# Corner taps summed on VectorE, rank-one lots beside contractions, and row stores in threads of their own

## The chip, the cores and the metric

The kernel runs on one core of a Trainium2 chip. Its engines work side by side, each through its own instructions in their order: TensorE (PE in the profile; PEld are its weight loads), VectorE (DVE), ScalarE (ACT), GpSimd (POOL) and SyncE (SP), whose queue issues most DMAs. They wait for one another by semaphores. The metric is the device time of one execution in microseconds (us); the kernel before took 39103.82 us in the median of three runs (39095.82 to 39139.67).

## The reference, cut to what matters

Two layers on an image batch of 8 × 128 × 64 × 64. The first adds a deformable convolution of the group-normalised image: for each of nine taps, four corners of the image are gathered, weighted and summed, and the taps are contracted with the convolution's weights.

```python
v = g(y0i, x0i) * ((1 - wy) * (1 - wx))[None] + g(y0i, x0i + 1) * ((1 - wy) * wx)[None] \
    + g(y0i + 1, x0i) * (wy * (1 - wx))[None] + g(y0i + 1, x0i + 1) * (wy * wx)[None]
...
out = jnp.einsum('bckhw,ock->bohw', cols, weight.reshape(Cout, Cin, K2))
```

The second takes the 4096 pixels of each image as a sequence. After a layer norm it runs a state-space scan with a state of 256 × 256 (d, n) per image, then a mixture of eight experts of which each pixel uses two.

```python
deltaA = jnp.exp(jnp.einsum('bld,dn->bldn', delta, A))
deltaB = jnp.einsum('bld,bln->bldn', delta, Bv)

def step(state, inp):
    dA_i, dB_i, x_i, C_i = inp
    state = dA_i * state + dB_i * x_i[:, None, :]
    y = jnp.einsum('bdn,bn->bd', state, C_i)
    return (state, y)
```

All of it is float32.

## The kernel before, in words

**Ahead of the scan** the kernel normalises the images, computes the offsets, and writes the table of corners (`table`), the gather indices and corner weights (`recs`) and the images themselves (`xl`) to DRAM.

**The scan** goes over 4096 positions, for all eight images at once. Sixteen positions are a *block* (256 of them), two are a *chunk* (eight a block), and one is a *step*. A hardware loop of eight turns holds 32 blocks, written out by `scan_block`. Each step has 12 *slots*; what is emitted in a slot is written out by hand, and it fixes each engine's order.

The state is kept transposed, n on the partitions, as four *pairs* of images of 1024 elements a partition: pairs 0, 1 and 2 in SBUF (`ht`), pair 3 in PSUM (`ud`). A step does this:

- `product` (L960) multiplies the decay factors `et` by the state: on GpSimd for pairs 0 to 2, into the four buffers `mt` that are used in turn (`buf`, L956: product p of step j has buffer (3j + p) mod 4), and on VectorE for pair 3, into the one buffer `md`.
- `unit` (L943) makes delta · B · x on TensorE, as rank-one lots from `uu`, into the one PSUM tile `up` (pairs 0 to 2) or added later to pair 3's own `ud`. `add` (L967) is VectorE's sum of product and lot. A new lot for `up` waits until the addition has read the one before.
- `contract` (L974) contracts a product with C (`zc`) on TensorE, into `yp`, 16 records for two pairs. It reads the products and not the new state; what B contributes is put in at the end of the block (`qt` in `behind`, L750). A buffer of `mt` is free for a later product when its contraction has read it.
- `decay` (L913) makes the decay factors of the chunk after this one: 19 groups of bf16 matmuls from `rt` (rows of delta, split into three bf16 parts, laid out with zeros) and `alhs` (rows of A), each into one of the PSUM banks that turn, and ScalarE's exponential (L933) from there into `et`. The groups are spread over slots 0 to 20 of a chunk's 24.

At the start of a chunk SP's queue gets the loads of `uu` for the next chunk (L897, four DMAs) and of `rt` for the one after that (L888, one DMA of 1102.5 KB). Both come from DRAM, where the scan's operands were stored a block ahead.

**Between these** the work of other blocks is dealt out by *threads* (Python generators that yield a number of slots): `conv` (L548) for the block two ahead, `project` (L623) for the next one, and `behind` for the one before. In each slot `Work.step` (L477) lets a thread emit its next piece while the planned load of TensorE and of VectorE is under ROOM (7.0, 9.0); every slot takes RATE (3.2, 3.2) off that load, and each piece adds its `cost`. Three banks are shared: a thread takes one (`take`) and gives it back (`free`), and the decays turn over the rest. Every thread must have ended when the block in which it runs ends.

- `conv` gathers a tap's four corners by an indirect DMA on GpSimd's queue (L567), scales them on ScalarE (L588, four operations into `w`), and sums and transposes them at once on TensorE, by four matmuls with the identity that add up in one bank (L596). ScalarE copies the result to `vt` (L603). After nine taps come the convolution and the layer norm.
- `project` makes delta, B · x, C and the gate. The three bf16 parts of delta and of B · x are stored to `pr` (L671 and L722, 12 DMAs each), and those of delta as rows to `rz` (L698: three parts of ten groups of rows, 30 DMAs), all on SP's queue, each lot at the point of `project` where its data is ready, the rows ten to a slot.

The order of the queue at the change, per block: chunk 1 has `uu` and `rt`, then 12 stores of `dpt` and 30 of `dst`; chunk 2 has its loads only; chunk 3 its loads and the 12 stores of `bpt`.

Of the kernel before, what the change touches and what calls it, by code (L numbers as in the profile page):

```python
# [32 lines left out]
P = 128  # L33
# [35 lines left out]
RATE = (3.2, 3.2)  # L69
# [4 lines left out]
def kernel(  # L74
# [352 lines left out]
    md = fix.tile([P, 2, NH, DIN], FP, name="md")  # L427
# [42 lines left out]
    class Work:  # L470
# [77 lines left out]
    def conv(b0, l0, kt):  # L548
# [13 lines left out]
        vt = one.tile([P, TAPS + 1, P], FP, tag="bulk", name="vt")  # L562
# [14 lines left out]
        for j in range(2):  # L577
            gather(j)
            yield 4
        for j in range(TAPS):  # L580
# [4 lines left out]
            w = two.tile([P, 4 * P], FP, name="w")  # L585
            for q in range(4):
                c0 = TAPS + 4 * j + q
                nc.scalar.activation(  # L588
                    w[:, P * q : P * q + P], g[:, P * q : P * q + P], AF.Copy,
                    scale=rec[:, c0 : c0 + 1],  # L590
                )
                yield 1
            yield 1
            wk = yield from take()
            for q in range(4):
                nc.tensor.matmul(  # L596
                    wk[:, :P], w[:, P * q : P * q + P], ident,
                    start=(q == 0), stop=(q == 3),
                )
# [22 lines left out]

    def project(k):  # L623


        wk = yield from take()
# [10 lines left out]
        z = one.tile([P, DIN], FP, name="z")  # L637
# [31 lines left out]
        for p in range(QI // 2):  # L669
            for i in range(3):  # L670
                nc.sync.dma_start(  # L671
                    out=pr[k].rearrange("i j p w b l n -> i p w (b l) j n")[i, p, 1],
                    in_=dpt[32 * p : 32 * p + 32],
                )
        yield 1
# [17 lines left out]
        for i in range(3):  # L693
            for a in range(NA + 1):
                q = min(GD, P - GD * a)
                c0 = 3 * i * NCH * RROW
                c1 = c0 + 3 * NCH * RROW
                nc.sync.dma_start(  # L698
                    out=rz[k][:q, c0:c1].rearrange("q (m x) -> q m x", x=RROW)[
                        :, :, 2 * a * CT : 2 * a * CT + 2 * CT  # L700
                    ],
# [417 lines left out]
```

## Time and profile before

| what | us |
|---|---|
| median of three runs | 39103.82 |
| the profiled execution | 39033.45 |
| its span, first to last instruction | 39031.8 |
| of it, before the scan's first product | 1771.5 |
| ScalarE's exponentials, L933 (40980 of 518 ns) | 19952.0 busy |
| VectorE's additions, L969 (12288 of 1218 ns) | 14971.8 busy |
| TensorE's decay matmuls, L924 | 12481.6 busy |
| TensorE's contractions, L981 from `mt` | 9369.2 busy |
| TensorE's lots, L949 into `up` | 5013.7 busy |
| mean granted TensorE clock | 0.949 |

Busy time counts what overlaps within a row once, and rows of one engine can overlap one another. The time of 39031.8 is one execution's; the median of the runs is 70 us above it. The page's slices are alike from the third of forty on: the scan repeats one block 256 times, so the block is the unit in which its time can be read. DMA engines are busy for about three tenths throughout, at 100 GB/s. A row's last part, after the second bar, is the time in which the engine stood idle just ahead of such instructions, and what ended that.

### The profile page before, as it was taken

How to read it: one execution, taken by the hardware profiler on the slowest of the kernel's cores; microseconds unless marked ns; L12 is line 12 of the kernel's file. 1: busy time of each engine (PE TensorE's matmuls, PEld its weight loads, DVE VectorE, ACT ScalarE, POOL GpSimd, SP SyncE). 2: the span in 40 equal slices, each digit the busy share in tenths (PEclk: the TensorE clock that was granted, in tenths of full speed). 3: DMA queues.
4: the chain of work that ended last, by engine and by line, in shares of the span. 5: the costliest groups of instructions: out<-in, count | busy, mean ns of one | idle time of the engine just before them, and what ended most of it. 6: DMA issues, size and time to landing. Idle time of an engine off the chain costs nothing. (4 is left out here: it accounts for less than half of the span.)

```text
span 39031.8 us, 851601 instructions
## 1 busy us (share of the span) xinstructions
PE 31598.8 (81%) x324270; PEld 17751.1 (45%) x324270; DVE 27353.8 (70%) x35860; ACT 24136.3 (62%) x62725; POOL 31028.9 (79%) x14691
## 2 busy tenths in 40 slices
PE   3488888888888888888888888888888888888888
PEld 1244444444444444444444444444444444444444
DVE  1277777777777777777777777777777777777777
ACT  0166666666666666666666666666666666666666
POOL 0288888888888888888888888888888888888888
PEclk7799999999999999999999999999999999999999
DMA  3333333333333333333333333333333333333333
GB/s 87 77 101 102 101 100 101 101 101 102 101 99 102 102 100 101 101 101 101 102 99 100 102 102 101 100 102 101 101 103 101 102 101 102 102 99 102 103 102 98
DMA packets 4799907, 3906.80 MB, mean 100 GB/s; under 512 B 3351549, under 2 KB 4378966, under 8 KB 4536022
## 3 DMA queue, kind: packets, MB, share of 16 engines
q1 hardware_dynamic: 4529962, 3182.00, 29.1%
q0 software_dynamic: 185760, 608.85, 5.6%
q10 hardware_dynamic: 80072, 61.51, 0.6%
q8 instruction: 2532, 41.48, 0.4%
q14 instruction: 1581, 12.95, 0.1%
HBM read 3268.71 MB, written 582.10 MB: 99 GB/s over the span
## 5 line engine op out<-in xcount | busy, mean ns | idle before, releaser
L961 POOL TENSOR_TENSOR mt<-et,ht 128x1024 f32<-128x1024 f32 x12288 | 28707.8, 2367 | 5843.1 <-ACT et L933 2895.4
L933 ACT ACTIVATE et<-bank 128x448 f32<-128x448 f32 (+1 forms) x40980 | 19952.0, 518 | 10189.4 <-PE bank L924 9662.8
L969 DVE TENSOR_TENSOR ht<-mt,up 128x1024 f32<-128x1024 f32 x12288 | 14971.8, 1218 | 9770.2 <-PE ud L949 5277.8
L924 PE MATMUL bank<-rt,alhs 126*128 126x224 bf16 (+1 forms) x81960 | 12481.6, 258 | 3161.1 <-ACT et L933 1504.4
L924 PEld LDWEIGHTS <-alhs 126*128 126x128 bf16 x81960 | 6844.7, 100 | 9068.6 <-issue 7073.1
L981 PE MATMUL yp<-mt,zc 128*32 128x256 f32 x98304 | 9369.2, 405 | 0.0
L949 PE MATMUL up<-uu 32*128 32x256 bf16 x49152 | 5013.7, 277 | 2504.2 <-DVE ht L969 2271.0
L961 DVE TENSOR_TENSOR md<-et,ud 128x1024 f32<-128x1024 f32 x4097 | 4977.7, 1215 | 81.6 <-PE yp L981 57.5
L971 DVE TENSOR_TENSOR ud<-md,ud 128x1024 f32<-128x1024 f32 x4096 | 5005.2, 1222 | 0.0
L981 PEld LDWEIGHTS yp<-mt,zc 128*32 128x32 f32 x98304 | 3474.3, 113 | 3350.9 <-issue 1742.2
L981 PE MATMUL yp<-md,zc 128*32 128x256 f32 x32768 | 4520.8, 396 | 0.0
L949 PEld LDWEIGHTS <-uu 32*128 32x128 bf16 x65536 | 1858.8, 92 | 4900.8 <-issue 4660.2
L588 ACT ACTIVATE w<-g,rec 128x128 f32<-128x128 f32 x9288 | 3602.4, 404 | 122.5 <-DMA rec<-recs 113.3
L596 PE MATMUL bank<-ident,w 128*128 128x128 f32 x18576 | 2966.7, 289 | 262.8 <-ACT w L588 118.2
L596 PEld LDWEIGHTS bank<-ident,w 128*128 128x128 f32 x18576 | 2371.3, 191 | 941.4 <-ACT et L933 648.3
L567 POOL DMA_INDIRECT g<-table,rec x2322 | 2262.4, 974 | 494.0 <-issue 259.7
L949 PE MATMUL ud<-uu 32*128 32x256 bf16 x16384 | 1670.2, 282 | 206.0 <-DVE md L961 202.8
L981 PEld LDWEIGHTS yp<-md,zc 128*32 128x32 f32 x32768 | 1661.1, 111 | 0.0
L603 ACT COPY vt<-bank 128x128 f32<-128x128 f32 x2322 | 614.9, 265 | 1090.8 <-PE bank L596 1090.7
L859 ACT ACTIVATE se<-bank,gate 128x128 f32<-128x128 f32 x2048 | 768.2, 377 | 392.7 <-PE bank L852 359.1
L298 POOL MEMSET xpad<- 128x66 f32 x8 | 1.2, 153 | 1227.8 <-POOLq L265 1227.8
L852 PE MATMUL bank<-ew_sb,tn2t 128*128 128x256 f32 x2048 | 726.4, 439 | 170.3 <-ACT et L933 126.4
(200 smaller groups left out, 16168.0 us busy)
## 6 DMA issues: line engine op xcount, KB each, us to landing
rt<-rz SPq DMA_DIRECT2D x2050, 1102.5 KB
uu<-pr SPq DMA_DIRECT2D x8196, 36.0 KB
pr<-dpt SPq DMA_DIRECT2D x3084, 48.0 KB
pr<-bpt SPq DMA_DIRECT2D x3084, 48.0 KB
rz<-dst SPq DMA_DIRECT2D x6939, 21.0 KB
g<-table,rec POOLq DMA_INDIRECT x2322
rec<-recs SPq DMA_DIRECT2D x2064, 2.8 KB
table<-xtok SPq DMA_DIRECT2D x256, 128.0 KB
```

Of the source, the lines that this page charges most:

```text
L567: nc.gpsimd.indirect_dma_start(out=g, out_offset=None, in_=table, in_offset=bass.IndirectOffsetOnAxis(ap=rec.bitcast(I32)[:, j : j + 1], a ...
L588: nc.scalar.activation(w[:, P * q : P * q + P], g[:, P * q : P * q + P], AF.Copy, scale=rec[:, c0 : c0 + 1],)
L596: nc.tensor.matmul(wk[:, :P], w[:, P * q : P * q + P], ident, start=(q == 0), stop=(q == 3),)
L852: nc.tensor.matmul(wk[:, :DIN], tn2t, ew_sb[:, DIN * hf : DIN * hf + DIN], start=True, stop=True,)
L859: nc.scalar.activation(se[:, ex, :], wk[:, P * j : P * j + P], AF.Copy, scale=gate[:, ex : ex + 1],)
L924: nc.tensor.matmul(ps[:, m * (NH * f + h) : m * (NH * f + h + 1)].rearrange("p (q t) -> p q t", q=n), alhs[:KR, g + f, P * h : P * h + P], ...
L933: nc.scalar.activation(ec[:, :, :, P * f + d0 : P * f + d0 + n], ps[:, m * f * NH : m * (f + 1) * NH].rearrange("p (h d t) -> p h t d", h= ...
L949: nc.tensor.matmul((up if p < QP else ud)[:, r, h], uu[c % 2][rows, 0, b % 2, lo, P * h : P * h + P], uu[c % 2][rows, 1, b % 2, lo, :], st ...
L961: (nc.gpsimd if p < QP else nc.vector).tensor_tensor(buf(j, p), et[c % 2][:, lo, PAIRS[p][0] : PAIRS[p][1] + 1 : 2], ht[p] if p < QP else ...
L969: nc.vector.tensor_tensor(ht[p], buf(j, p), up, ALU.add)
L971: nc.vector.tensor_tensor(ud, md, ud, ALU.add)
L981: nc.tensor.matmul(yp[32 * (b // 2) : 32 * (b // 2) + 32, :DIN], zc[c % 2].rearrange("p s x -> p (s x)")[:, s0 : s0 + 32], buf(j, p)[:, r, ...
```

## The change

1. **Corner taps.** Of the nine taps, those with even number (five) are summed over their four corners by VectorE into `v` and transposed by one TensorE transpose. The odd ones keep their four matmuls. Two taps share a bank and one ScalarE copy, so there are five copies of `vt` and not nine. `vt` has a tile of its own.
2. **RATE** is (2.8, 3.2) and was (3.2, 3.2): TensorE's planned load is taken down more slowly, and background work is dealt out more thinly.
3. **Slots.** The lots of pairs 0 and 3 move from slot 3 to slot 2, ahead of the last step's contraction of pairs 1 and 2, which moves from slot 0 to slot 2 along with GpSimd's third product. The contraction of pairs 0 and 3 moves from slot 6, behind the lot of pair 1, to slot 9, behind the lot of pair 2. `md` has two buffers.
4. **Stores.** The stores of `dpt`, `dst` and `bpt` become threads, put ahead of the other threads three slots after their data is made; each issues three DMAs and yields three slots. Assertions check that a load is emitted only after all stores of what it reads. `z` and `bx` share one buffer.

```diff
-RATE = (3.2, 3.2)
+RATE = (2.8, 3.2)
...
-    md = fix.tile([P, 2, NH, DIN], FP, name="md")
+    md = several(2, [P, 2, NH, DIN], FP, "md")
...
+            while later:
+                self.threads.insert(0, [later.pop(0), slot])
...
+            ws[j] = two.tile([P, 4 * P], FP, name="w")
             for q in range(4):
...
+                if q == 1 and j % 2 == 1:
+                    nc.vector.tensor_reduce(
+                        v, ws.pop(j - 1).rearrange("p (q c) -> p c q", q=4), AX.X, ALU.add
+                    )
+                    cost(0, 5)
                 yield 1
+            if j % 2 == 0 and j + 1 < TAPS:
+                continue
+            n = 1 + j % 2
+            if n == 1:
+                yield 1
+                nc.vector.tensor_reduce(
+                    v, ws.pop(j).rearrange("p (q c) -> p c q", q=4), AX.X, ALU.add
+                )
+                cost(0, 5)
+                yield 2
             yield 1
             wk = yield from take()
-            for q in range(4):
-                nc.tensor.matmul(
-                    wk[:, :P], w[:, P * q : P * q + P], ident,
-                    start=(q == 0), stop=(q == 3),
-                )
-                cost(1)
-                if q == 1:
-                    yield 1
-            nc.scalar.copy(vt[:, j, :], wk[:, :P])
+            nc.tensor.transpose(wk[:, :P], v, ident)
+            cost(1)
+            if n == 2:
+                yield 1
+                w = ws.pop(j)
+                for q in range(4):
+                    nc.tensor.matmul(
+                        wk[:, P : 2 * P], w[:, P * q : P * q + P], ident,
+                        start=(q == 0), stop=(q == 3),
+                    )
+                    cost(1)
+                    if q == 1:
+                        yield 1
+            nc.scalar.copy(
+                vt[:, j + 1 - n : j + 1, :],
+                wk[:, : n * P].rearrange("p (t c) -> p t c", t=n),
+            )
...
+    def store_rows(k, dst):
+        yield LAG
+        for a in range(NA + 1):
+            q = min(GD, P - GD * a)
+            for i in range(3):
                 c0 = 3 * i * NCH * RROW
                 c1 = c0 + 3 * NCH * RROW
                 nc.sync.dma_start(
...
+            yield 3
+        there.add(("rows", k))
...
-                    if sl == 0:
+                    if sl == 2:
+                        unit(c, lo, (0, 3))
                         if last:
                             contract(*last.pop())
                         product(j, c, lo, 2)
                     elif sl == 3:
-                        unit(c, lo, (0, 3))
                         add(j, 0)
                     elif sl == 5:
                         add(j, 3)
                     elif sl == 6:
                         unit(c, lo, (1,))
-                        contract(j, c, lo, (0, 3))
...
                             product(*nxt, 3)
                         unit(c, lo, (2,))
+                        contract(j, c, lo, (0, 3))
```

`store_delta` and `store_b` have the same form as `store_rows`, with four rounds of three DMAs where that has ten.

More of the change, by code (lines that the diff above doesn't have):

```diff
@@ L561, in conv @@
         yield LOADS
-        vt = one.tile([P, TAPS + 1, P], FP, tag="bulk", name="vt")
+        vt = one.tile([P, TAPS, P], FP, name="vt")
         gs, ws = {}, {}
@@ L579, in conv @@
             yield 4
+        v = one.tile([P, P], FP, name="v")
         for j in range(TAPS):
@@ L636, in project @@
         yield 1
-        z = one.tile([P, DIN], FP, name="z")
+        z = one.tile([P, DIN], FP, tag="zb", name="z")
         nc.scalar.mul(z, wk[:, DIN:], 0.5)
@@ L668, in project @@
         free()
[L669 to L675, printed above, removed]
+        later.append(store_delta(k, dpt))
         dst = one.tile([P, 3, NCH, 2, CT], BF, name="dst")
@@ L692, in project @@
         free()
[L693 to L701, printed above, removed]
-                    in_=dst[GD * a : GD * a + q].rearrange("q j c f t -> q (j c) (f t)"),
-                )
-            yield 1
+        later.append(store_rows(k, dst))
+        yield 1
         wk = yield from take()
@@ L713, in project @@
         yield 1
-        bx = one.tile([P, DIN], FP, name="bx")
+        bx = one.tile([P, DIN], FP, tag="zb", name="bx")
         nc.scalar.copy(bx, wk[:, :DIN])
@@ L719, in project @@
         free()
-        for p in range(QI // 2):
-            for j in range(3):
-                nc.sync.dma_start(
-                    out=pr[k].rearrange("i j p w b l n -> j p w (b l) i n")[j, p, 0],
-                    in_=bpt[32 * p : 32 * p + 32],
-                )
+        later.append(store_b(k, bpt))
         yield 1
@@ L887, in load_r @@
     def load_r(k, c):
+        assert ("rows", k) in there
         nc.sync.dma_start(
@@ L895, in load_u @@
     def load_u(k, c):
+        assert ("delta", k) in there and ("b", k) in there
         for p in range(QI // 2):
@@ L1044, in run @@
             pass
+        while later:
+            run(later.pop(0))
     for b0 in range(0, NB, QI):
```

39 lines of the change are left out of this document (35 added, 4 removed).

## The prediction

> **What bounds it now.** I read the page first, then the waits, then one block of the scan cut at its eight chunks, then the queue that feeds it. Busy shares and three rows of the page:
>
> ```profile
> PE 31598.8 (81%) x324270; PEld 17751.1 (45%) x324270; DVE 27353.8 (70%) x35860; ACT 24136.3 (62%) x62725; POOL 31028.9 (79%) x14691
> L961 POOL TENSOR_TENSOR mt<-et,ht 128x1024 f32<-128x1024 f32 x12288 | 28707.8, 2367 | 5843.1 <-ACT et L933 2895.4
> L596 PE MATMUL bank<-ident,w 128*128 128x128 f32 x18576 | 2966.7, 289 | 262.8 <-ACT w L588 118.2
> L567 POOL DMA_INDIRECT g<-table,rec x2322 | 2262.4, 974 | 494.0 <-issue 259.7
> ```
>
> TensorE and GpSimd are both near 80%, so neither alone sets the time; the waits between them do:
>
> ```profile
> DVE ht L969 <- PE ud L949: 5277.8, 2864, 15.5
> POOL mt L961 <- ACT et L933: 2895.4, 1274, 32.5
> PE up L949 <- DVE ht L969: 2271.0, 3027, 1.9
> POOL mt L961 <- PE yp L981: 1284.1, 784, 6.0
> PE bank L924 <- DMA rt<-rz: 1256.3, 254, 11.7
> ```
>
> (Total us, times, longest.) Divided by 256 blocks, GpSimd loses 11.3 us a block to late decay factors (et) and 5.0 to a multiplicand buffer that TensorE has not read yet (yp); TensorE loses 8.9 to state additions that still hold `up`, and 4.9 to one load of `rt`. A block in the middle, its chunks from first product to first product (columns: us, then busy us of PE, PEld, DVE, ACT, POOL, TensorE clock, DMA share, GB/s):
>
> ```profile
> 22156.30:22173.50 17.20, 14.50 (x152) 8.14 (x151) 13.24 (x21) 11.43 (x30) 14.01 (x7) 1.00 0.29 82
> 22173.50:22191.60 18.10, 14.91 (x147) 7.86 (x147) 14.91 (x21) 10.86 (x26) 14.96 (x7) 0.91 0.39 115
> 22191.60:22208.50 16.90, 13.13 (x144) 6.56 (x143) 15.14 (x31) 10.53 (x26) 15.96 (x8) 1.00 0.54 87
> 22208.50:22231.70 23.20, 17.63 (x161) 9.05 (x162) 12.39 (x13) 12.78 (x34) 15.12 (x8) 0.85 0.45 137
> 22231.70:22250.70 19.00, 16.86 (x177) 10.61 (x176) 12.54 (x12) 12.82 (x35) 15.92 (x8) 1.00 0.33 99
> 22250.70:22268.30 17.60, 16.00 (x181) 9.28 (x179) 12.76 (x11) 14.16 (x40) 16.95 (x9) 1.00 0.36 112
> 22268.30:22283.80 15.50, 14.34 (x154) 9.48 (x154) 10.73 (x10) 11.67 (x31) 13.99 (x7) 1.00 0.28 92
> 22283.80:22299.80 16.00, 12.34 (x151) 7.04 (x149) 13.89 (x23) 9.70 (x24) 14.00 (x6) 1.00 0.25 82
> sum 143.50, PE 119.73 PEld 68.03 DVE 105.61 ACT 93.94 POOL 120.92; mean PE 14.97 PEld 8.50 DVE 13.20 ACT 11.74 POOL 15.12
> ```
>
> This block's 143.5 us stand for 256 (37225 us from the first product at 1771.5 to the end of the last, 145.4 each with the loop's turns). Six products keep GpSimd 14.0 us in every chunk; the chunks last 15.5 to 23.2. The worst, chunk 3, starts with the wait for `rt`. The timeline of the queue and of TensorE shows why:
>
> ```profile
> 22190.50 13.85 SPq L698 DMA_DIRECT2D rz<-dst  x30
> 22204.44 1.35 SPq L897 DMA_DIRECT2D uu<-pr  x4
> 22206.42 0.32 SPq L888 DMA_DIRECT2D rt<-rz  x1
> 22212.40 0.55 PE L924 MATMUL bank<-rt,alhs 126*128 126x224 bf16 x2 [4.34 <-DMA rt<-rz]
> ```
>
> Thirty row stores take SP 13.85 us; the loads that chunk 2 should issue first thing (22191.6) stand behind them, and `rt` is issued 14.8 us into the chunk. It lands some 6 us later (22206.42 to 22212.40), when TensorE has stood 4.34 us.
>
> **The change, part by part.** The sum is made per chunk. I count each engine's instructions between the first rank-one lots of successive chunks in the order in which they stand in both built programs, and price them by rows.
>
> *TensorE.* A 128-column float32 matmul is 0.32 us (L596: 2966.7 over 9288 matmuls of two records), a 256-column one 0.70 (L543, wb: 358.5 over 514). Background matmuls by chunk stand, narrow/wide, at 7/2, 6/0, 0/2, 12/4, 19/2, 12/0, 19/0, 1/2 before: 76 × 0.32 + 12 × 0.70 = 32.7 us. The scan's share is then 119.7 - 32.7 = 87.0, or 10.9 a chunk. Each of five taps loses four matmuls (2966.7/2322 = 1.28 us) for one transpose (L618: 84.8/258 = 0.33 us), so 4.7 us a block go. With RATE 2.8 the rest is spread: 7/2, 4/0, 7/2, 5/0, 4/6, 16/0, 16/0, 2/2. TensorE by chunk: 14.5, 12.8, 12.3, 17.5, 18.4, 14.7, 17.0, 12.6 before, 14.5, 12.2, 14.5, 12.5, 16.4, 16.0, 16.0, 12.9 after.
>
> *GpSimd.* 14.0 a chunk and 1.19 a gather ((2262.4 + 494.0)/2322). The nine gathers stand 0, 1, 2, 1, 2, 3, 0, 0 before and 0, 1, 4, 1, 2, 1, 0, 0 after, so chunk 2 rises to 18.8.
>
> *VectorE.* Five reductions of 512 elements a partition are new, and no row has one: a reduction of 256 (L747) is 0.425, an addition of 1024 (L969) 1.218; these are the ends. It is nearest to L747; on the line between them it is 0.69, so 3.4 us a block (2.1 to 6.1). Chunks 2 to 6, where they stand, have 1.8 to 10.8 us of idle VectorE before; the cover is there. Without it 3.4 × 256 = 880 us come on. The gate's small operations move into chunk 3, which then holds ten large ones (12.2), seventeen of about 0.21 and one reduction: 16.5, more than GpSimd's 15.2. Chunk 7 gets three small ones more: 13.9 + 0.7 = 14.6.
>
> [...]
>
> *The larger of the three engines,* chunk by chunk: before 14.5, 15.2, 16.4, 17.5, 18.4, 17.6, 17.0, 14.0, sum 130.6; after 14.5, 15.2, 18.8, 16.5, 16.4, 16.0, 16.0, 14.6, sum 128.0. The block took 143.5, so 12.9 were waits: by chunk 2.7, 2.9, 0.5, 5.7, 0.6, 0, -1.5, 2.0 (the negative one is work TensorE had left over or done early).
>
> *Stores as threads.* The count is the same, 12 + 30 + 12, at 0.46 us each (13.85/30), but three at a time, so that a load finds at most a few ahead. Chunk 1 issues 6, chunk 2 27 and chunk 3 21; 27 × 0.46 = 12.4 us in a chunk of some 18, so SP keeps up. The loads of chunk 2 now stand ahead of all row stores, those of chunk 3 behind at most two threes (2.8 us); with 2 us of `uu` and 6 of landing `rt` is there 11 us into a chunk of 17. I take the wait out: 4.3 of chunk 3's 5.7. Bounds: all of 4.9, and nothing if the stores, which are still in the same queue, hold the loads elsewhere; a loss is excluded by their unchanged count. Chunk 3's clock (0.85) should go back to 1.00 with the stall; that I leave uncounted, the prices being means.
>
> *Rank-one lots beside contractions.* Before, a contraction stands between the lots of pairs 2 and 0 and one between those of 1 and 2; afterwards one stands behind the lots of 0 and 3 and one behind that of 2. TensorE then has 1.07 us of work while VectorE adds the pair just made. At most the whole wait on `up` goes, 8.9 us a block. Against it, the contraction of pairs 0 and 3 moves from slot 6 to slot 9, behind the lot of pair 2, and the next step's second product overwrites that buffer 2.33 us into the step. Third additions begin late: 1.4, 4.5, 3.2, 4.4, 3.1, 0.8, 0.1 and 3.2 us after their product ended, in the first steps of the eight chunks (start of L969 against the end of its product, mean over 240 blocks). Add 1.1 for the contraction, and every lateness over 1.2 would hold GpSimd: 0.2 + 3.3 + 2.0 + 3.2 + 1.9 + 2.0 = 12.6 us a block, were all of it on the path. It is not, since where TensorE is late, GpSimd waits for et at the chunk's end anyway, and there the contraction now stands behind the last decays, which come 1.07 earlier. I take a net gain of 1.0. The second `md` buffer takes away 57.5 us in the whole run, and four vt copies fewer are on ScalarE, idle over 3 us a chunk: both nothing.
>
> *Sum.* After: the larger engine plus the old excess, without rt: 17.2, 18.1, 19.3, 17.9, 17.0, 16.0, 14.5, 16.6 = 136.6, less 1.0 = 135.6, which is 7.9 below 143.5. Over 256 blocks 2022 us; 39033 - 2022 = 37011 on the profiled execution. The median of the runs is 70 above it (39104), so 37080.
>
> **Rivals.** *Waits melt too.* An even load also empties half of what then still lies over 128.0, 3.8 us a block: 11.7 × 256 = 2995, 36110. For it: the waits on `up` and on banks are found in loaded chunks. Against: chunks 0 and 7 are hardly lightened.
>
> *The rt wait only moves.* Stores and loads share one queue, and stores now go on into chunk 3. If 4.9 us a block come back, 3.0 × 256 = 768 are won: 38340. Against it: 12.4 us of stores in 18.
>
> *The second product is held* (slower). One mechanism: slot 9's contraction behind the lot of pair 2, at a price of up to 12.6 us a block. All of it on the path gives 143.5 - 7.9 + 12.6 = 148.2, or 40310. It decides from 63% on (7.9/12.6). For it: additions are 3 to 4 us late in five of eight chunks. Against: TensorE, which causes the lateness, is relieved by 4.7 and 4.3 us.
>
> **How the numbers follow.** Forecast 0.53, melted waits 0.17, rt moved 0.14, held product 0.16. The time is the forecast's, 37080. The range reaches down past the melted case to 35900 (about 0.05 below) and up past the moved wait, to the forecast with about half the hold on the path (38700), at 38800 (about 0.15 above). A measurement tells 0.2% from no change, some 80 us. Only the held product is slower: 0.16; 0.02 of the moved wait falls within 0.2%; 0.82 is faster.
>
> **What would show it.** The row of waits for rt near zero, no 13 us run of row stores in the queue, and TensorE's clock at 1.00 in chunk 3. Some 6.4 us a block fewer (5 × 1.28) on the four-matmul taps, and five reductions near 0.69 in each block, with GpSimd's product still at 2.37. Chunk 2 the longest, near 19, chunk 3 down to 18. GpSimd's wait for yp below 1284. I am wrong if that row grows past 2000 us with GpSimd's second product at its end, or if the rt wait stays above 600, or if VectorE becomes busy more than 95% in chunk 3 and TensorE waits there.

## The result, and the profile after

The changed kernel takes 40281.44 us in the median of four runs (40246.94 to 40313.86), the kernel before 39099.82 beside it: a ratio of 1.0301, with an interval of 1.0283 to 1.0318. It is slower by 3%, where 5% faster was forecast. The profiled execution has a span of 40312.2 us and a mean granted clock of 0.924 (before: 0.949).

From the page of the kernel after, the busy shares and the rows that answer to those shown of before, with the new reduction:

```profile
PE 32271.1 (80%) x315240; PEld 17515.7 (43%) x315240; DVE 28663.1 (71%) x37150; ACT 24002.8 (60%) x61693; POOL 31196.9 (77%) x14691
...
L1014 POOL TENSOR_TENSOR mt<-et,ht 128x1024 f32<-128x1024 f32 x12288 | 28854.4, 2365 | 7005.6 <-PE yp L1034 4925.3
...
L621 PE MATMUL bank<-ident,w 128*128 128x128 f32 x8256 | 1536.4, 317 | 1.0 <-ACT w L593 0.9
...
L598 DVE TENSOR_REDUCE v<-w 128x128 f32<-128x512 f32 x1032 | 1074.1, 1041 | 51.8 <-ACT w L593 23.4
```

TensorE issues 9030 records fewer and is busy 672 us longer. The taps did get cheaper (2966.7 to 1536.4 us), so something else got dearer: the same matmuls last longer. GpSimd's product is unchanged at 2365 ns. The waits after:

```profile
DVE ht L1022 <- PE ud L1002: 4962.7, 2661, 15.8
POOL mt L1014 <- PE yp L1034: 4925.3, 3822, 5.7
...
PE up L1002 <- DVE ht L1022: 1745.2, 1993, 2.4
POOL mt L1014 <- ACT et L986: 1466.2, 1387, 34.7
...
PE bank L977 <- DMA rt<-rz: 12.1, 1, 12.1
```

The wait for `rt` is gone (1256.3 to 12.1 us). GpSimd's wait for a buffer that TensorE has yet to read grew from 1284.1 to 4925.3, and its wait for decay factors fell by 1429. One block, cut at its chunks as before, and below it chunk 6 of another block of the same run:

```profile
16822.90:16843.80 20.90, 17.04 (x159) 9.24 (x160) 14.01 (x15) 11.73 (x30) 14.08 (x6) 0.92 0.22 66
16843.80:16862.70 18.90, 15.07 (x144) 7.72 (x144) 14.39 (x26) 10.31 (x25) 15.08 (x7) 0.91 0.29 86
16862.70:16881.50 18.80, 14.72 (x162) 7.82 (x165) 14.66 (x18) 13.37 (x36) 17.99 (x10) 1.00 0.69 167
16881.50:16896.70 15.20, 11.57 (x134) 5.74 (x123) 14.80 (x28) 11.21 (x30) 15.00 (x7) 1.00 0.64 162
16896.70:16918.60 21.90, 18.92 (x163) 10.53 (x162) 14.17 (x17) 12.07 (x31) 16.11 (x9) 0.85 0.22 74
16918.60:16936.60 18.00, 16.20 (x170) 9.40 (x169) 11.97 (x11) 12.23 (x31) 15.12 (x8) 1.00 0.30 97
16936.60:16955.80 19.20, 15.96 (x146) 8.52 (x147) 13.26 (x12) 12.95 (x36) 14.04 (x6) 0.82 0.24 75
16955.80:16973.10 17.30, 14.10 (x158) 8.52 (x158) 13.52 (x24) 9.61 (x24) 14.16 (x7) 1.00 0.23 76
...
22945.90:22962.40 16.50, 13.42 (x147) 7.11 (x147) 13.26 (x12) 12.63 (x36) 14.05 (x6) 1.00 0.29 87
```

Chunk 3 has shrunk from 23.2 to 15.2, as hoped. But where the clock stood at 1.00 in all chunks but two, it now dips in four. The two lines for chunk 6 hold the same work, and VectorE and GpSimd are busy equally long in them; with the clock at 0.82 TensorE is busy 15.96 us and the chunk takes 19.20, at 1.00 it is busy 13.42 and the chunk takes 16.50. TensorE's timeline in that slower chunk 6 shows the dip:

```profile
16939.86 1.07 PE L1034 MATMUL yp<-mt,zc 128*32 128x256 f32 x16
16940.87 0.75 PE L977 MATMUL bank<-rt,alhs 126*128 126x224 bf16 x6
16941.87 0.35 PE L977 MATMUL bank<-rt,alhs 126*128 126x224 bf16 x2 [0.26 <-ACT et L986]
16942.16 0.39 PE L1002 MATMUL up<-uu 32*128 32x256 bf16 x4
16942.59 0.35 PE L977 MATMUL bank<-rt,alhs 126*128 126x224 bf16 x2
16943.32 0.35 PE L977 MATMUL bank<-rt,alhs 126*128 126x224 bf16 x2 [0.37 <-DVE ud L1024]
16944.04 0.33 PE L615 MATMUL bank<-ident,v 128*128 128x128 f32 x1 [0.37 <-ACT et L986]
16944.76 0.53 PE L977 MATMUL bank<-rt,alhs 126*128 126x224 bf16 x2 [0.39 <-ACT et L986]
16945.23 0.61 PE L1002 MATMUL up<-uu 32*128 32x256 bf16 x4
...
16947.63 1.22 PE L621 MATMUL bank<-ident,w 128*128 128x128 f32 x4
```

The contraction of slot 2 ends at about 16940.9. Until the one of slot 9 TensorE has only decay matmuls at ScalarE's pace, lots and one transpose: busy by its records for most of the time, but thinly. From 16944.44 (so the clock's own record in the trace) everything is slower: two decay matmuls 0.53 and not 0.35, four lots 0.61 and not 0.39, and two matmuls of a tap (four records, x4 in the line) 1.22, where the same four records take 0.71 at full clock (in the other chunk 6, at 22955.68). The record ends at 16951.26, 6.83 us or twice 3.41 later.

The clock's records in the traces before and after have two values only, 1.0 and 0.5, and change on a grid of 3.41 us. In the scan before there are 526 stretches at 0.5, 11.5 us a block, nearly all from steps 2 and 6 on (in 6 stands the wait for `rt`); after, 1054, 19.9 us a block, in chunks 0, 1, 3 to 7. Sorted by whether a chunk has more than 0.3 us of half clock in it, over the 240 blocks after that are neither the first nor the last of a loop turn:

```
chunk                       0      1      2      3      4      5      6      7
blocks with half clock     98%    53%     5%    39%    65%    32%    81%    44%
us, at full clock        18.39  17.72  18.81  15.24  19.34  17.95  16.56  17.26   sum 141.3
us, with half clock      21.43  18.89  19.67  16.43  20.68  18.99  18.72  20.65
us, mean                 21.36  18.34  18.85  15.70  20.21  18.29  18.31  18.76   sum 149.8
us, mean, before         17.18  18.63  16.92  24.10  19.03  17.60  15.55  16.00   sum 145.0
```

By these lines the block would take 8.5 us less at full clock. That is only a sorting, and in chunk 0 a thin one: its 18.39 comes from five blocks, each the second of a loop turn. The experiments test it.

### The profile page after: what moved, and what is told of

It is laid out like the page before. It is cut to its first block, busy times and chain, and to the rows that moved or that the text cites. A ratio compares the mean times of both kernels' runs of the same rounds, so it can differ in the third digit from the quotient of the medians.

```text
span 40312.2 us, 834847 instructions
## 1 busy us (share of the span) xinstructions
PE 32271.1 (80%) x315240; PEld 17515.7 (43%) x315240; DVE 28663.1 (71%) x37150; ACT 24002.8 (60%) x61693; POOL 31196.9 (77%) x14691
## 5 line engine op out<-in xcount | busy, mean ns | idle before, releaser
L1014 POOL TENSOR_TENSOR mt<-et,ht 128x1024 f32<-128x1024 f32 x12288 | 28854.4, 2365 | 7005.6 <-PE yp L1034 4925.3
L1022 DVE TENSOR_TENSOR ht<-mt,up 128x1024 f32<-128x1024 f32 x12288 | 14972.5, 1218 | 9744.4 <-PE ud L1002 4962.7
L977 PE MATMUL bank<-rt,alhs 126*128 126x224 bf16 (+1 forms) x81960 | 12772.5, 258 | 3147.4 <-ACT et L986 2653.6
L977 PEld LDWEIGHTS <-alhs 126*128 126x128 bf16 x81960 | 7168.6, 101 | 9519.2 <-issue 8865.5
L1002 PE MATMUL up<-uu 32*128 32x256 bf16 x49152 | 5195.2, 281 | 1824.3 <-DVE ht L1022 1745.2
L1034 PE MATMUL yp<-md,zc 128*32 128x256 f32 x32768 | 5077.8, 435 | 0.0
L1014 DVE TENSOR_TENSOR md<-et,ud 128x1024 f32<-128x1024 f32 x4097 | 4969.6, 1213 | 21.8 <-ACT et L986 21.8
L621 PE MATMUL bank<-ident,w 128*128 128x128 f32 x8256 | 1536.4, 317 | 1.0 <-ACT w L593 0.9
L621 PEld LDWEIGHTS bank<-ident,w 128*128 128x128 f32 x8256 | 1243.1, 216 | 358.7 <-issue 350.5
L598 DVE TENSOR_REDUCE v<-w 128x128 f32<-128x512 f32 x1032 | 1074.1, 1041 | 51.8 <-ACT w L593 23.4
L545 PE MATMUL bank<-wconv_sb,vt 128*128 128x128 f32 x4644 | 863.9, 335 | 0.7 <-ACT vt L628 0.7
```

The lines of the kernel that those rows point to most:

```text
L545: nc.tensor.matmul(ps_out, lhs, rhs, start=(i == 0), stop=(i == n - 1))
L598: nc.vector.tensor_reduce(v, ws.pop(j - 1).rearrange("p (q c) -> p c q", q=4), AX.X, ALU.add)
L621: nc.tensor.matmul(wk[:, P : 2 * P], w[:, P * q : P * q + P], ident, start=(q == 0), stop=(q == 3),)
L977: nc.tensor.matmul(ps[:, m * (NH * f + h) : m * (NH * f + h + 1)].rearrange("p (q t) -> p q t", q=n), alhs[:KR, g + f, P * h : P * h + P], ...
L1002: nc.tensor.matmul((up if p < QP else ud)[:, r, h], uu[c % 2][rows, 0, b % 2, lo, P * h : P * h + P], uu[c % 2][rows, 1, b % 2, lo, :], st ...
L1014: (nc.gpsimd if p < QP else nc.vector).tensor_tensor(buf(j, p), et[c % 2][:, lo, PAIRS[p][0] : PAIRS[p][1] + 1 : 2], ht[p] if p < QP else ...
```

## The experiments

Times are medians, ratios are to the kernel before beside it. "Half clock" is the time at clock 0.5 per block of the scan, and a wait per block is its total divided by 256, both from the trace.

### First: what each part does

**Product buffers.** The changed kernel with five `mt`, paid for by three gather buffers for four and a shared tile for `dpt` and `bpt`.

```diff
-    mt = several(4, [P, 2, NH, DIN], FP, "mt")
+    mt = several(5, [P, 2, NH, DIN], FP, "mt")
...
-        return mt[(QP * j + p) % 4] if p < QP else md[j % 2]
+        return mt[(QP * j + p) % 5] if p < QP else md[j % 2]
```

> The changed kernel with five product buffers in place of four, so that no product waits for the contraction of the step just before until its own third turn (room is made by three gather buffers in place of four and one buffer for the stored parts of delta and B). Theory H (GpSimd's products are held by contractions that stand later): the wait of products for yp falls from 4925 us to under 1500 and the time to 36700 to 38300. Theory C (contractions now stand 7 and 5 slots apart in place of 6 and 6, so stretches without one let TensorE's clock drop to half, 1068 stretches in place of 537): the wait for yp falls too, the mean clock stays at 0.91 to 0.93, and the time stays over 39600. Theory V (five reductions of 1.04 us in VectorE's queue make the additions late): time over 39600 as well, clock undecided.

40660.72 us, 1.0400 (1.0383 to 1.0417). GpSimd's wait for `yp` did go, to 1.3 us a block, but its wait for `et` rose to 15.9, half clock stayed (21.2), and the time rose. So removing the hold in this way wins nothing. The way has a price of its own, the gather buffer and the shared tile, and no run has that price alone.

**Slots alone**, in the kernel before (with the second `md`, `vt` without its spare row):

```diff
-                    if sl == 0:
+                    if sl == 2:
+                        unit(c, lo, (0, 3))
                         if last:
                             contract(*last.pop())
...
-                        contract(j, c, lo, (0, 3))
                     elif sl == 7:
...
                         unit(c, lo, (2,))
+                        contract(j, c, lo, (0, 3))
```

> The kernel before with the new slots and two md buffers alone. H: the time rises to 40600 to 42300 (8 to 12.6 us a block) with the wait for yp over 4000. C: it rises to 40300 to 41500 with a clock under 0.93 and over 900 stretches of half clock. V: no change, 39100 within 300, since no reduction is in it.

38903.34 us, 0.9950 (0.9934 to 0.9967). GpSimd's wait for `yp` rose here too, to 12.5 us a block, and half clock to 13.3, yet the kernel got a little faster. That is what was expected if the slots by themselves cost nothing; the theories of the hold and of the clock had both forecast a loss. TensorE's wait for `rt` fell as well, from 1256 to 466 us.

**Half of the slots back:** in the changed kernel the contraction of pairs 0 and 3 goes back to slot 6.

```diff
                         unit(c, lo, (1,))
+                        contract(j, c, lo, (0, 3))
...
                         unit(c, lo, (2,))
-                        contract(j, c, lo, (0, 3))
```

> The changed kernel with the contraction of pairs 0 and 3 back in slot 6, behind the lot of pair 1; the other stays in slot 2, so that they stand 4 and 8 slots apart. H: the second product is no longer held by slot 9, the wait for yp falls to about 2500 and the time to 38300 to 39200. C: the longer stretch without a contraction makes the clock no better (0.92 or lower, 1000 stretches or more) and the time stays at 39900 to 41500. V: no change, 40280 within 300.

39770.05 us, 1.0173 (1.0156 to 1.0190), half clock 21.8: between the ranges and in none of them. The wait for `yp` fell by nearly half (2657.8 us), and 511 us came back although half clock rose. Chunk 0, at half clock in 98% of the changed kernel's blocks, meets it in none here and takes 18.01 us where it took 21.36; chunk 2 meets it in all and takes 24.05 where it took 18.85.

**RATE back** in the changed kernel.

```diff
-RATE = (2.8, 3.2)
+RATE = (3.2, 3.2)
```

> The changed kernel with RATE back at 3.2. Theory R (the thinner dealing costs: background matmuls are spread so thinly that TensorE's clock drops to half more often, and a thread holds a bank in every step, so that decays turn over two): the time falls to 38000 to 38900, stretches of half clock to under 750 (from 1068), and decays' wait for ScalarE to free a bank from 2654 us to under 1900. Theory T (the corner taps cost: five reductions of 1.04 us among the additions, and fewer dense matmuls): the time stays at 39800 to 40600.

39900.99 us, 1.0206 (1.0189 to 1.0223), half clock 24.9: 380 us of the 1182 lost come back, and not by the time at half clock, which rose. In the changed kernel, then, the thinner dealing is not what brings half clock.

**Taps alone:** the kernel before with part 1 of the change, the new `conv`, and nothing else of it.

> The kernel before with the corner taps' reductions, transposes and shared copies alone. T: the time rises to 39700 to 40700, with more stretches of half clock than 537. R: the time stays at 38600 to 39200, a little better for 4.7 us of matmuls fewer in a block.

39096.75 us, 0.9997 (0.9987 to 1.0007). Level, as one theory had it, and with the half clock that the other had forecast: chunks 3 and 4 are 3.8 us shorter by the mean, while chunks 5, 6 and 7, at half clock never or in 2% of blocks before, meet it now in 94%, 30% and 59% of blocks (half clock 19.7 us a block).

**Stores alone:** the kernel before with part 4 of the change, the new `project` and its threads, and nothing else of it.

> The kernel before with the stores in threads of their own alone. If the wait for rt lay on the path, as the prediction has it, it falls from 1256 us to under 300 and the time to 37800 to 38500. If it was hidden or only moves, the time stays at 38900 to 39400. R and T both leave this open.

40670.06 us, 1.0396 (1.0379 to 1.0413), above both ranges: the part that takes the `rt` wait away loses most. Half clock is 26.9 us a block. Chunk 6 takes 23.4 us at half clock (96% of blocks) and 17.4 without. In the block of this kernel that stands at the same place, chunks 5 and 6, and TensorE's timeline at the end of chunk 6:

```profile
17068.90:17085.30 16.40, 15.20 (x177) 8.87 (x176) 12.47 (x11) 13.81 (x40) 16.06 (x9) 1.00 0.29 96
17085.30:17108.40 23.10, 19.11 (x162) 12.10 (x158) 11.26 (x13) 11.30 (x29) 13.97 (x7) 0.78 0.21 66
```

```profile
17093.68 1.23 PE L598 MATMUL bank<-ident,w 128*128 128x128 f32 x4 [0.20 <-ACT et L959]
...
17099.98 1.81 PE L1007 MATMUL yp<-mt,zc 128*32 128x256 f32 x16
```

The last taps and the convolution now fall into a stretch at half clock: 1.23 us for four records (two matmuls) that take 0.71 at full clock, 1.81 for a contraction of 1.07.

**Slots back:** the changed kernel with lots and contractions in their old slots (the diff of the slots reversed), and

```diff
-RATE = (2.8, 3.2)
+RATE = (2.85, 3.2)
```

> The changed kernel with lots and contractions in their old slots (RATE 2.85; at 2.8 the threads do not end in their block). Theory H (products held by contractions that stand later) as it stood: 36900 to 37900. R and T, after the new slots alone came out 200 us faster than before: no gain, 40000 to 40900.

38712.60 us, 0.9900 (0.9884 to 0.9917), half clock 20.3: between the two ranges. So three parts of four, with more half clock than before, win 1%, and no part adds up with another: the slots alone win 200 us, but taking them out of the change wins 1570. (With RATE at 2.8 and the old slots there is no time: a block's threads do not end in it.) The hold is nearly gone here:

```profile
POOL mt L1014 <- PE yp L1034: 530.9, 523, 2.2
```

GpSimd's wait for `et` is 4488.7 us instead. The time at half clock is as long as in the change, but it stands elsewhere: in chunk 0 in 12% of blocks (17.00 us by the mean, 21.36 in the change), in chunk 4 in none (18.22 against 20.21), and in chunks 1, 2 and 3 in 97%, 93% and 80%. So the time at half clock is no price by itself, and this run can't tell what the hold and what the place of half clock had cost.

### Second: the clock by itself

If half clock follows from thin TensorE work and costs the time, then *added* work that does nothing must make the kernel faster. `warm` puts matmuls of a full 128 × 128 weight on zeros into the gap; they add zero to `yp`.

```diff
+    zero = fix.tile([P, DIN], BF, name="zero")
+    nc.vector.memset(zero, 0.0)
...
+    def warm(n):
+        for _ in range(n):
+            nc.tensor.matmul(
+                yp[:, :DIN], alhs[:, 0, :P], zero, start=False, stop=False
+            )
...
+                    if sl in (5, 7) and j0 > 1:
+                        warm(2)
                     work(NSLOT * j0 + sl)
```

> The changed kernel plus dead work on TensorE: in slots 5 and 7 of steps 2 to 15, in the long gap between the contraction of slot 2 and that of slot 9, two matmuls each of a full 128x128 weight on 256 zero bfloat16 columns, added into the sums of the contraction (they add zero). 56 of them per block; successive decay matmuls of 224 columns start 0.09 to 0.12 us apart in the timeline and stand at 0.267 us in the rows, so 6 to 15 us of TensorE per block. Clock theory (a stretch of 3.41 us in which the array is less than about half used drops TensorE to half clock for the next 3.41 us; this is what the change brought, 19.9 us per block at half clock against 11.5 before): half clock falls below 12 us per block and the time falls, although work is added, to 38,700 to 39,900 us. Work theory (TensorE simply has too little room in the order of the change, the clock follows from its stalls and costs nothing): half clock stays near 20 us per block and the time goes up to 40,600 to 41,900 us.

39103.95 us, 0.9994 (0.9984 to 1.0004). Added work, and 1177 us less: the whole loss is gone. Half clock fell from 19.9 to 6.2 us a block, and most of what is left (5.1) stands in steps 0 and 1, which got no `warm`. Its page and its windows of chunks 4 to 6:

```profile
PE 31810.3 (81%) x329576; PEld 18181.2 (46%) x329576; DVE 28648.4 (73%) x37151; ACT 24009.4 (61%) x61693; POOL 31213.7 (80%) x14691
...
L1052 PE MATMUL yp<-zero,alhs 128*128 128x256 bf16 x14336 | 2745.9, 272 | 0.0
```

```profile
16433.60:16452.90 19.30, 16.73 (x171) 10.07 (x170) 14.05 (x17) 12.12 (x31) 16.07 (x8) 1.00 0.26 85
16452.90:16471.10 18.20, 16.71 (x179) 10.17 (x180) 11.96 (x11) 12.34 (x31) 15.13 (x8) 1.00 0.29 96
16471.10:16487.50 16.40, 13.98 (x155) 7.79 (x155) 13.24 (x12) 12.61 (x36) 14.07 (x6) 1.00 0.30 87
```

TensorE has 14336 matmuls more than after and is busy 461 us less. Chunk 6 is 16.40 us, where the same block took 19.20.

**Tap work put back as dead work:** three float32 matmuls of constants behind each transpose of a VectorE sum.

```diff
             nc.tensor.transpose(wk[:, :P], v, ident)
             cost(1)
+            for q in range(3):
+                nc.tensor.matmul(
+                    wk[:, 2 * P : 3 * P], ident, win_sb[:, :P], start=True, stop=True
+                )
```

> The changed kernel with the TensorE work that the corner taps lost put back as dead work: behind each transpose of a VectorE sum, three float32 matmuls of the identity on 128 columns of constants, written where nothing reads them; the VectorE sums stay. 15 per block, 15 x 0.32 = 4.8 us at most. Clock theory: the taps run in chunks 5 to 7 and their dense matmuls had kept the clock up there; half clock in chunks 5 to 7 falls by more than half (now 32%, 81% and 44% of blocks), time 39,300 to 40,100 us. Work theory: 40,300 to 41,400 us.

39713.96 us, 1.0156 (1.0139 to 1.0173), half clock 12.2: none left in chunks 6 and 7 (81% and 44% of blocks without the dead work). In chunk 5, where a fall was expected too, it rose from 32% to 59%. In chunks 6 and 7, then, such work keeps the clock up; for chunk 5 this run does not show it.

**Twice the dose:**

```diff
-                        warm(2)
+                        warm(4)
```

> As the first, with four dead matmuls instead of two in each of the two slots: 112 per block, 12 to 30 us of TensorE. Clock theory: half clock below 6 us per block; the time is at or below that of the smaller dose where half clock was still left there, and above it where it was not: 38,500 to 40,300 us. Work theory: 41,800 to 43,500 us.

39326.47 us, 1.0053 (1.0036 to 1.0069), half clock 4.3. Little half clock was left in steps 2 to 15, and the second dose costs 222 us against the first.

**Old slots and `warm(2)`,** in the long gap that stands there:

```diff
-                    if sl in (5, 7) and j0 > 1:
+                    if sl in (2, 4) and j0 > 1:
```

> The changed kernel with the lots and contractions in their old slots (38,713 us, 20.3 us per block at half clock) plus the same dead matmuls, two each in slots 2 and 4, in the long gap between the contractions of slots 0 and 6. Clock theory: half clock below 11 us per block, time 37,700 to 38,500 us. Work theory: half clock stays, time 38,900 to 40,300 us.

38068.24 us, 0.9733 (0.9716 to 0.9749), half clock 8.5 (RATE is 2.85 here too): 644 us less than without the dead work.

### Third: where the rest of the forecast went

**The kernel before with the same `warm(2)`** in slots 2 and 4:

> The kernel before plus the same dead matmuls as with the old slots (two each in slots 2 and 4 of steps 2 to 15): how much of its own time is half clock that filler can take away, so that change and before can be compared with the clock cared for on both sides. Its 11.5 us per block at half clock stand almost all in steps 2 and 6, behind TensorE waits (the rt load in step 6) in which nothing behind in its queue can run. If so, half clock stays at 8 to 11.5 us per block and the time at 38,900 to 39,300 us. If filler takes it away: below 5 us per block and 38,000 to 38,700 us, and the change is then no better than before at any clock.

39375.62 us, 1.0071 (1.0055 to 1.0088), half clock 12.3, both just above the first range. Before does not gain: its half clock stays in steps 2 and 6, where TensorE waits, and dead matmuls that stand behind the waiting one did not fill the gap. So this run does not give the kernel before at full clock.

**Five products and `warm(2)`** in the changed kernel (the zeros 128 columns wide, four matmuls for two):

> The changed kernel with the dead matmuls (39,104 us, GpSimd waiting 14.5 us per block for contractions to free product buffers) and a fifth product buffer, paid for by one gather buffer less and one shared staging tile. Hold theory, with the clock out of the way: the new slots' late contractions keep the products' buffers and swallow the rest of the expected gain: 38,000 to 38,700 us. Rival: the freed GpSimd waits for exponentials instead, as without the dead matmuls (40,661 against 40,281 us): 39,000 to 39,600 us.

39545.53 us, 1.0114 (1.0097 to 1.0131), half clock 8.1. As in the first try, the wait for `yp` goes (0.3 us a block) and waits for `et` take its place (16.4). A fifth buffer at this price does not help with less half clock either.

**Stores alone with `warm(2)`** in slots 2 and 4:

> The kernel before with the stores as threads alone (40,670 us, 26.9 us per block at half clock) plus the dead matmuls, two each in slots 2 and 4. Clock theory: the stores' move costs nothing by itself and its loss is half clock: half clock below 13 us per block, time 38,500 to 39,400 us. Store theory (the transfers or the reordered background work are late by themselves): half clock may fall, but the time stays at 40,200 to 41,200 us.

39067.15 us, 0.9992 (0.9983 to 1.0002), half clock 9.3. The loss of the stores, 1570 us, goes with the half clock.

**Old slots, more where half clock was left:**

```diff
-                        warm(2)
+                        warm(4 if j0 < 8 or j0 == 15 else 2)
```

> The best so far (lots and contractions in their old slots, with dead matmuls, 38,068 us, 8.5 us per block still at half clock, in steps 2 to 7 and 15) with four dead matmuls instead of two in each slot of steps 2 to 7 and 15. Clock theory: half clock below 6 us per block, 37,600 to 38,000 us. If TensorE's room is used up: 38,100 to 38,700 us.

37836.38 us, 0.9678 (0.9662 to 0.9694), half clock 4.5: the fastest version here, 3.2% below before and 6.1% below the change (37836/40281).

**`warm` in steps 0 and 1 too:** four matmuls of 64 columns behind each decay group of those steps, in the spare columns of its bank.

```diff
+        if c == 1 and g < NG - 1:
+            for _ in range(4):
+                nc.tensor.matmul(
+                    ps[:, NH * m :], alhs[:, 0, :P], zero[:, : 512 - NH * m],
+                    start=True, stop=True,
+                )
         ec = et[c % 2].rearrange(
```

> The changed kernel with the dead matmuls (39,104 us) has none in steps 0 and 1, and there 98% of its blocks still drop to half clock: chunk 0 takes 21.7 us in those and 18.4 us in the others. Here steps 0 and 1 get theirs too: behind each decay group of these steps four matmuls of a full weight on 64 zero columns, into the spare columns of the group's own bank. Clock theory: chunk 0 falls to 18.4 to 19.5 us and the time by 256 x 2.2 to 3.3 us, to 38,250 to 38,550 us; so most of what the new slots still cost against the old ones (38,068 us with dead matmuls) is half clock. Slot theory: GpSimd's and VectorE's waits for late contractions and lots make chunk 0 long by themselves, and the time stays at 38,900 to 39,400 us.

39602.29 us, 1.0126 (1.0109 to 1.0143), above both ranges: a miss. Chunk 0 still met half clock in 94% of blocks. The thin stretch there lies ahead of these matmuls, at the turn from step 15, where TensorE stands 2.13 us for an addition in the block looked at; and ScalarE's exponential now waits for the dead matmuls in the same bank (1609 us in all). The 18.4 us that were hoped for are those of the few second blocks of a loop turn. It says nothing of what the slots cost by themselves.

**The same count on a sixteenth of the array:**

```diff
-                yp[:, :DIN], alhs[:, 0, :P], zero, start=False, stop=False
+                yp[:32, :DIN], alhs[:32, 0, :32], zero[:32], start=False, stop=False
```

> The same 56 dead matmuls per block on 256 columns, in the same slots, but of a weight of 32 rows and 32 columns, a sixteenth of the array. If the clock goes by how much of the array works (columns x passes x rows x columns of the weight), these hold nothing up: half clock stays at 17 to 21 us per block and the time at 40,000 to 40,800 us. If any instruction keeps the clock up: below 12 us per block and 39,000 to 39,500 us.

41537.53 us, 1.0621 (1.0604 to 1.0639), half clock 22.7. The same instructions in the same slots, 273 ns each as the full ones (272), do not keep the clock up, and the kernel is slower still, by 1256 us than without them. Between this run and the first of this part only the size of the weight differs: half clock 22.7 against 6.2 us a block, time 41538 against 39104. So half clock cost time here, and it did not go by the count or the length of TensorE's instructions. Half clock and time of this control lay above what I expected of it.

## Why the prediction was wrong

**The step that failed** is one sentence: "Chunk 3's clock (0.85) should go back to 1.00 with the stall; that I leave uncounted, the prices being means." The clock in chunk 3 did go back (half clock in 39% of blocks, all of them before). But I priced every TensorE instruction at its mean and put a change of the clock at nothing, when the clock goes by each stretch of the order: taps alone, stores alone and, a little, slots alone raised half clock (19.7, 26.9 and 13.3 us a block from 11.5). In the changed kernel it is 19.9, and dead work that brings it to 6.2 takes 1177 us off, 4.6 us a block, while the same dead work on a small weight does not. That is the loss: without it the change is level with before (0.9994).

It is not the whole error. Level with before means that the forecast gain of 7.9 us a block (39104 against 37080) did not come either, and for that the clock is at most in part to blame. Two more terms failed, the larger engine of a chunk and the gain of the slots (below). Nor is half clock a loss wherever it stands: taps alone have as much of it as the change and lose nothing, and the change in its old slots has 20.3 us of it and is 1% faster than before. What then decides may be where it falls and what waits for TensorE there; no experiment here shows that.

**Part by part.**

- *The rt wait* was right: 4.9 us a block to 0.05. But "a loss is excluded by their unchanged count" was wrong. The stores alone cost 1570 us, though no DMA was added; as threads they shift the background work behind them, and in the block shown half clock falls where taps and convolution stand. With dead work 1603 us came back, all of the loss.
- *Taps.* TensorE's time for them fell nearly as worked out, 2966.7 to 1949.7 us with the transposes (1536.4 + 413.3), 4.0 us a block against 4.7; with dead work and less half clock it is 1760.2, and the fall 4.7. The kernel's time did not fall: alone the taps moved nothing, since most of what chunks 3 and 4 gained went in chunks 5 to 7, which now meet half clock. In the changed kernel, putting work back cleared chunks 6 and 7 of it.
- *Reductions* were mis-sized: 1041 ns and not 690, inside the bounds (425 and 1218) and nearer to the other end. Their cover was nearly used up: VectorE is busy 14.80 of 15.20 us in chunk 3 of the block shown, 97%, past the 95% named as a sign of being wrong. But that is the chunk that became shorter than forecast.
- *The larger engine of a chunk.* It foresaw 17.0, 16.0 and 14.5 us for chunks 4, 5 and 6, shortened by 2.0, 1.6 and 1.0 because TensorE was relieved. In blocks without half clock there they take 19.34, 17.95 and 16.56, and with dead work 19.34, 18.15 and 16.54, so some 2 us a chunk are missing with the clock cared for. Busy time of the largest engine, with the old excess added, was no bound that is met; which wait fills the rest stays open. Chunks 1 and 2 were near (18.1 and 19.3 against 17.72 and 18.81), chunk 3 was 2.7 us better. The largest miss is chunk 0, 21.36 by the mean against 17.2, at half clock in 98% of blocks.
- *Lots and contractions.* A gain of 1.0 was taken. In the old slots the change with dead work is 1036 us faster than in the new (38068 against 39104, with RATE at 2.85), 4.0 us a block. More than all of that stands in chunk 0 (21.6 us against 17.0), at half clock in the one and hardly in the other. How much of it is the clock, the experiment on steps 0 and 1 did not tell, and it stays open; with the slots alone, chunk 0 takes 17.69 in the 181 of 240 blocks without half clock there, against 17.18 before.

**The rivals.** The measured time, 40281, is close to the rival of the held product (40310), and its sign shows: GpSimd's wait for `yp` rose to 4925 us, past the 2000 that I had named. But its mechanism, the hold as the price by itself, does not stand. With the slots alone the wait is 3197 us and the kernel is faster than before; taking the hold away by a fifth buffer (at the price of a gather buffer) made the kernel slower twice; and giving TensorE dead work, which left 3710 us of that wait standing, took the whole loss away. Against that, putting the contractions back, half or whole, removed the wait and 511 or 1570 us without less time at half clock, so a share of the hold in the changed kernel is not ruled out. That the number came so near is luck: in the two runs with a fifth buffer the wait's removal was not worth its size. The rival that the rt wait only moves fell with its row (12.1 us), and that waits melt too (36110) was farthest off.

**How thin is too thin.** I cut the scan into the stretches of 3.41 us on which the clock's records lie, and for each at full clock added up what its matmuls used of the array: columns, times the share of the array that the weight covers (the array taken as the 128 × 128 cells of the largest weight in the records), a float32 column counted twice (four contraction matmuls of 256 columns, on a quarter of the array each, start within 0.03 us of one another and the next four 0.215 us later; two dead bf16 ones of 256 start 0.113 us apart), against the columns that fit into the stretch at 0.42 ns each (0.215 us / 512). How many stretches were followed by half clock:

```
use of the array      before          after           with warm(2)     on 1/16 array
under 0.30            403 of 403      355 of 355      246 of 246       666 of 666
0.30 to 0.35          107 of 107      429 of 429       51 of  51       319 of 397
0.35 to 0.40           16 of  77      270 of 658       19 of 342       107 of 468
0.40 and more           0 of 9451       0 of 8336       0 of 9812        0 of 8396
```

One limit near 0.37 sorts all but 5 of 10038 stretches before and 35 of 9778 after. These two counts hang on how the matmuls are laid on the grid (moved by 50 ns against it they are 16 and 75); that all under 0.30 and none from 0.40 on led to half clock does not. With the small dead matmuls the middle rows are mixed more (319 of 397, 107 of 468). By TensorE's busy time the stretches can't be sorted, since after, the middle half of those that led to half clock were 58% to 67% busy, and 5% of the others were under 66%. Of the 204 that led to half clock in step 13, none was under 58% busy. The sorting is read from traces; that a full weight in place of a small one, with the same number of instructions of the same length, moves the clock and the time is shown by the two runs with dead matmuls (half clock 6.2 and 22.7 us a block, 39104 and 41538 us). The limit at about half of the array, with which I expected the first run with `warm`, was a guess, and too high.

## What to carry to other kernels

Where the profile's clock is below 1.00, read it per stretch before pricing anything, and ask of each change what it does to the *thinnest* 3.41 us of TensorE and not only to its sum: work removed or spread out there can cost more than it saves (of the 1182 us that the change lost, dead work in such stretches took 1177 off). Dead matmuls of a full weight are a cheap test of it, and in the old slots a gain of 644 us too; in the kernel before they cost some 280. A wait that grows beside a loss is not yet its cause; take it away and look. And the time at half clock is not a price list either: the same 20 us of it went with 38713 us in one order and with 40281 in another.

## What the runs showed of the hardware

In the traces of these kernels TensorE's granted clock was 1.0 or 0.5, for whole stretches of 3.41 us; half clock followed every stretch that used under 0.30 of the array and none that used 0.40 or more, in each of the four traces above. A matmul of a 32 × 32 weight took as long in the records as one of 128 × 128 (273 and 272 ns) and left 22.7 us of half clock a block where the large one left 6.2. VectorE's sum of 512 float32 to 128 took 1.04 us, nearly as long as an addition of 1024 (1.22).
